# States on the partitions in a selective scan: state sums by few-column matmuls, delta*u spread by DMA

## The chip, the cores and the metric

The kernel runs on one core of a Trainium2 chip. The metric is the time on the device in microseconds (us), lower is better. Lines such as L342 are lines of the kernel before. PE is the matmul engine (PEld its weight loads), DVE, ACT and POOL are the vector, scalar and GpSimd engines, SP issues the transfers.

## What is computed

The input is 8 images of 96 channels and 64x64 positions. A layer of group norm, layer norm, in_proj, depthwise convolution and Silu gives 192 inner channels per image. Then comes the selective scan, over 4096 positions in each of four directions (by rows, by columns, and both reversed), with 16 states per channel. In the reference, cut to this:

```python
def step(h, t):
    u_t, d_t, B_t, C_t = t
    dA = jnp.exp(d_t[..., None] * A)
    h = dA * h + (d_t * u_t)[..., None] * B_t[:, :, None, :]
    y = jnp.einsum('bkdn,bkn->bkd', h, C_t)
    return (h, y)
```

Here `u` is the convolved image in the direction's order, `d` (delta) is a softplus of a low-rank projection of u, B and C are projections of u to 16 values per position, and A is a constant per direction, channel and state. The four directions' y are put back into the image's order and added, with D*u; then follow a norm over the 192 channels, a gate, out_proj and the residual, attention without softmax, and a quantised FFN. All of the scan is in float32.

## The kernel before, in words

The images are handled in four pairs, one after the other, each in four stages: `front` (norms, in_proj, convolution), `scan`, `back` (norm, gate, out_proj), `tail` (attention, FFN). Two images share three tiles of 128 partitions with channels on the partitions: tile 0 is channels 0 to 127 of image 0, tile 1 the same of image 1, tile 2 the last 64 channels of both.

`scan` (L229) goes over 32 steps, four directions times 8 chunks of 512 positions. A step has three tiles T and 16 states n, and each (step, T, n) is a unit; a pair has 1536 units, and a unit's work has 128 channels on the partitions and 512 positions along the free dimension:

- `unit_a` (L318): two bf16 matmuls with a selection matrix spread row n of B and of C over the partitions (L322, L324). ACT makes `da = exp(delta * A)` with A as a per-partition scale (L326). DVE multiplies B by delta*u in PSUM (L329). ACT copies C to SBUF (L331).
- `unit_b` (L336): DVE's scan instruction gives the states h (L342), POOL multiplies them by C (L344), ACT keeps the last column for the next chunk (L347).
- `unit_c` (L350): PE adds the 16 states' products into one PSUM bank with an identity matrix (L352); after the 16th, DVE adds the bank to the running sum of the directions in SBUF (L357, L362).

The units are software-pipelined by hand (L369 to L390): `unit_a` of unit i, `unit_b` of i-1, `unit_c` of i-3. The projections of the next step (`project`, L260; `step_size`, L281, with softplus put together from Relu, Abs, Exp and Ln and three POOL operations) are put in between. In the columns' directions, `view` (L239) reads the image with a stride of 64 elements. All data between the steps stays in SBUF; SP has almost nothing to do in the scan: the weights `xw` and `dtw` of each direction (L256, L258).

`back` reads the sum y and the gate z chunk by chunk; `mix` (L400) forms means over the 192 channels with matrices that respect the three-tile layout. In `back`, po is made of a matmul with 128 rows (L442) and one with 64 rows (L443), the latter on partitions 0 to 63 for image 0 and 64 to 127 for image 1. `tail` holds f32 matmuls with few columns: `pk` (L486, 192 columns), `pm` (L495, 96 columns). At the start, L50 loads the constants, among them `sel` (128 rows of 12,288 bytes), `wkv` (97 rows of 768 bytes), `alog` (128 of 512) and `gmat` (96 of 384), before x is loaded (L139).

Of the kernel before, what the change touches and what calls it, by code (L numbers as in the profile page):

```python
# [30 lines left out]
HG = 4  # L31
LOGEXP = "natural_log_exp_and_others"

# Two images share three 128-partition tiles of the 192 inner channels:
#   tile 0: image 0, channels 0..127      tile 1: image 1, channels 0..127
#   tile 2: channels 128..191 of image 0 (partitions 0..63) and of image 1 (64..127)
# [3 lines left out]
def vss_attn_ffn(ctx: ExitStack, tc: tile.TileContext, a: dict):  # L40
# [12 lines left out]
    # one table set for all but Silu  # L53
# [10 lines left out]
    c192 = load("c192", [128, 6, 128])  # L64
    j192 = load("j192", [128, 6, 128])
    sel = load("sel", [128, 3, NS, 128], BF16)
# [4 lines left out]
    inb = load("inb", [128, 2, 2])  # L71
# [3 lines left out]
    ds = load("ds", [128, 2, KD])  # L75
    onw = load("onw", [128, 2])
    onb = load("onb", [128, 2])
    woT = load("woT", [128, 2, DIM])
# [6 lines left out]
    # A = -exp(A_log); the sum over the directions of D, as all four read the same u  # L85
    amat = load("alog", [128, KD, 2, NS])
    nc.scalar.activation(amat, amat, AF.Exp)
    nc.vector.tensor_scalar(amat, amat, -1.0, None, ALU.mult)
    dsum = const.tile([128, 2], F32, name="dsum")
    nc.vector.tensor_reduce(dsum, ds, mybir.AxisListType.X, ALU.add)  # L90

    # FFN weights and biases in the 5-bit exponent, 2-bit mantissa format
# [26 lines left out]
    def front(pair, xi, zs, ybuf):  # L119
        with ExitStack() as st:  # L120
# [53 lines left out]
            # Silu from here on, in a table set of its own  # L174
            for b in range(2):
                xt = xts[b]
                lo = slice(64 * b, 64 * b + 64)
                for c in range(NCH):
                    cs = bass.ts(c, F)
                    r0 = c * ROWS  # L180
                    for j in range(2):
                        pm = ps.tile([128, F], F32, name="pm", tag="ps")
                        nc.tensor.matmul(
                            pm, winT[:, j * DI : j * DI + 128], xt[:, cs], start=True, stop=True
                        )
                        pl = ps.tile([128, F], F32, name="pl", tag="ps")
                        nc.tensor.matmul(
                            pl[lo], winT[:, j * DI + 128 : (j + 1) * DI], xt[:, cs],
                            start=True, stop=True,
                        )  # L190
                        if j == 0:
                            nc.scalar.activation(
                                pad[b][:, r0 + 1 : r0 + 1 + ROWS, 1 : HH + 1],
                                pm.rearrange("p (h w) -> p h w", w=HH),
                                AF.Identity, bias=inb[:, 0, 0:1],
                            )
                            nc.scalar.activation(
                                pad[2][lo, r0 + 1 : r0 + 1 + ROWS, 1 : HH + 1],
                                pl[lo].rearrange("p (h w) -> p h w", w=HH),
                                AF.Identity, bias=inb[lo, 0, 1:2],  # L200
                            )
                        else:
                            zt = tmp.tile([128, 2, F], F32, name="zt")
                            nc.scalar.activation(zt[:, 0], pm, AF.Silu, bias=inb[:, 1, 0:1])
                            nc.scalar.activation(
                                zt[lo, 1], pl[lo], AF.Silu, bias=inb[lo, 1, 1:2]
                            )
                            nc.sync.dma_start(zs[b, :, cs], zt[:, 0])
                            nc.sync.dma_start(zs[2, lo, cs], zt[lo, 1])

            for T in range(3):
                for c in range(NCH):
# [9 lines left out]
                    silu = nc.scalar.activation(  # L222
                        xi[T][:, bass.ts(c, F)], pc, AF.Silu, bias=convb[:, half(T) : half(T) + 1]
                    )
            with tc.issue_after(silu.ins):
                nc.scalar.preload_act_table_set(LOGEXP)

# [1 line left out]
    def scan(xi, y):  # L229
        with ExitStack() as st:  # L230
            wk = st.enter_context(tc.tile_pool(name="wk", bufs=2))
            pr = st.enter_context(tc.tile_pool(name="pr", bufs=1))
            wt = st.enter_context(tc.tile_pool(name="wt", bufs=3))
            psb = st.enter_context(tc.tile_pool(name="psb", bufs=3, space=PSUM))
            psc = st.enter_context(tc.tile_pool(name="psc", bufs=2, space=PSUM))
            psy = st.enter_context(tc.tile_pool(name="psy", bufs=2, space=PSUM))
            psm = st.enter_context(tc.tile_pool(name="psm", bufs=1, space=PSUM))

            def view(t, k, c):  # L239
                """Chunk c of an image in the order of direction k (before its flip)."""  # L240
                if k % 2 == 0:
                    return t[:, bass.ts(c, F)].rearrange("p (h w) -> p h w", w=HH)
                return t.rearrange("p (h w) -> p w h", w=HH)[:, bass.ts(c, ROWS), :]

            def rows(t):
                return t.rearrange("p (h w) -> p h w", w=HH)

            steps = []
            for k in range(KD):
                order = range(NCH) if k < 2 else range(NCH - 1, -1, -1)  # L250
                steps += [(k, c, i == 0) for i, c in enumerate(order)]
            xw, dtw, S, dts, delta, du = {}, {}, {}, {}, {}, {}

            def weights(k):
                xw[k] = wk.tile([128, 2, 3, 128], F32, name="xw")
                nc.sync.dma_start(xw[k], a["xw"][k])  # L256
                dtw[k] = wk.tile([128, 3, 128], F32, name="dtw")
                nc.sync.dma_start(dtw[k][32:44], a["dtw"][k])  # L258

            def project(s, g):  # L260
                """B (g = 0, with the step's low rank) or C: rows 0..31, 64..95 and 96..127 of S
                get the high, middle and low bfloat16 parts, whose sum is the float32 value."""
                k, c, _ = steps[s]
                if g == 0:
                    S[s] = pr.tile([128, 2, F], BF16, name="S", bufs=2)
                pt = psm.tile([128, F], F32, name="pt", tag="m")
                for T in range(3):
                    nc.tensor.matmul(  # L268
                        pt, xw[k][:, g, T, :], view(xi[T], k, c), start=(T == 0), stop=(T == 2)
                    )  # L270
                Sg = S[s][:, g]
                nc.scalar.activation(Sg, pt, AF.Copy)  # L272
                R = pr.tile([128, F], F32, name="R")
# [32 lines left out]
            def feed(s, T):  # L306
                """What must have run before tile T of step s, in parts."""
                if s >= len(steps):
                    return []
                k, _, first = steps[s]  # L310
                parts = []
                if T == 0:
                    if first:
                        weights(k)
# [368 lines left out]
```

## Time and profile before

| what | value |
|---|---|
| median of 3 runs | 16,712.39 us (16,696.8 to 16,720.28) |
| span of the profiled execution, first to last instruction | 16,699.4 us; it lies among the three runs, and no other time of it is given |
| `front` of the first pair, up to its first projection | 430 us |
| `scan` of the first pair | 3359 us |
| `back` of the first pair | about 130 us |
| busy share of DVE, PE, POOL, ACT | 76%, 84%, 59%, 59% |
| instructions of PE | 32,636 matmuls and as many weight loads |
| data moved by DMA | 106 MB, 6 GB/s over the span |

A group's row reads: line, engine, operation, output <- inputs, shape, count | busy us, mean ns of one | idle time of the engine just before them and what ended it. A window's row gives each engine's busy time in that stretch, then the granted share of PE's clock, the share of the 16 DMA engines that was busy, and GB/s. A row of the waits names who waited for whom, us in total, how often, and the longest.

### The profile page before, as it was taken

The numbers are of one execution on the slowest core, as the hardware profiler recorded it, in microseconds if no ns is written. First come the engines' busy times: TensorE is split into PE (matmuls) and PEld (weight loads), VectorE is DVE, ScalarE is ACT, GpSimd is POOL, SyncE is SP. The second block draws the span as 40 slices with busy tenths as digits, with TensorE's granted clock in tenths as the row PEclk, the third lists the DMA queues.
The fourth block names the chain that finished last, engine by engine and source line by source line (L and its number), as shares of the span: only waits on it lengthen the run. The fifth ranks groups of instructions, "written<-read, shape, count | busy, mean of one in ns | idle before, by whom it ended". The sixth has DMA issues, their size and how long they took to land. (4 is left out here: it accounts for less than half of the span.)

```text
span 16699.4 us, 126308 instructions
## 1 busy us (share of the span) xinstructions
PE 14068.0 (84%) x32636; PEld 4820.2 (29%) x32640; DVE 12648.8 (76%) x14809; ACT 9813.3 (59%) x17754; POOL 9871.6 (59%) x7738
## 2 busy tenths in 40 slices
PE   8888888888988888888898888888889888888888
PEld 2222222223222222222332222222233222222223
DVE  0898899883189889988318988998830898899883
ACT  2666666663266666666326666666632666666663
POOL 0677777772067777777106777777710677777771
PEclk9999999997799999999779999999977999999997
DMA  1000000000000000000000000000000000000001
GB/s 31 2 2 1 2 1 1 1 1 29 24 2 2 1 1 1 1 1 0 30 24 2 2 0 2 1 1 1 1 30 26 0 2 0 2 1 1 1 1 31
DMA packets 48735, 106.06 MB, mean 6 GB/s; under 512 B 7075, under 2 KB 7940, under 8 KB 47108
## 3 DMA queue, kind: packets, MB, share of 16 engines
q1 hardware_dynamic: 48004, 97.97, 2.0%
q8 instruction: 256, 4.19, 0.1%
q14 instruction: 475, 3.89, 0.1%
HBM read 60.21 MB, written 37.75 MB: 6 GB/s over the span
## 5 line engine op out<-in xcount | busy, mean ns | idle before, releaser
L344 POOL TENSOR_TENSOR hc<-h,cc 128x512 f32<-128x512 f32 x6144 | 7831.6, 1280 | 3405.2 <-DVE h L342 2561.7
L352 PE MATMUL py<-hc,ident 128*128 128x512 f32 x12288 | 7244.3, 673 | 1992.9 <-POOL hc L344 1968.2
L342 DVE TENSOR_TENSOR_SCAN h<-da,st,pb 128x512 f32<-128x512 f32 x5376 | 6839.4, 1272 | 11.3
L331 ACT ACTIVATE cc<-pcc 128x512 f32<-128x512 f32 x6144 | 3665.9, 597 | 3446.6 <-POOL hc L344 2798.5
L329 DVE TENSOR_TENSOR pb<-pb,du 128x512 f32<-128x512 f32 x6144 | 4184.9, 681 | 1296.2 <-PE pb L322 1268.9
L326 ACT ACTIVATE da<-delta,c_alog 128x512 f32<-128x512 f32 x6144 | 4414.6, 719 | 497.2 <-DVE h L342 461.7
L352 PEld LDWEIGHTS py<-hc,ident 128*128 128x128 f32 x12288 | 2131.0, 202 | 4978.2 <-POOL hc L344 4475.7
L322 PE MATMUL pb<-S,c_sel 128*128 128x512 bf16 x6140 | 2449.9, 399 | 145.1 <-DVE h L342 141.8
L324 PE MATMUL pcc<-S,c_sel 128*128 128x512 bf16 x6144 | 2348.9, 398 | 5.2 <-POOL S L279 2.5
L279 POOL TENSOR_TENSOR S<-R,S 32x512 bf16<-32x512 f32 x256 | 295.7, 1155 | 1838.5 <-DVE S L278 948.1
L324 PEld LDWEIGHTS <-c_sel 128*128 128x128 bf16 x6144 | 628.6, 102 | 2303.6 <-issue 2250.3
L274 DVE TENSOR_TENSOR R<-pt,S 64x512 f32<-64x512 f32 x256 | 177.8, 695 | 1307.3 <-ACT S L272 1300.0
L322 PEld LDWEIGHTS <-c_sel 128*128 128x128 bf16 x6144 | 631.4, 103 | 1777.1 <-issue 1772.9
L268 PE MATMUL pt<-xi,xw 128*128 128x512 f32 x1536 | 1125.5, 825 | 21.1 <-DMA xw<-in_xw_dram 9.9
L342 DVE TENSOR_TENSOR_SCAN h<-da,pb 128x512 f32<-128x512 f32 x768 | 924.6, 1209 | 5.9
L217 PE MATMUL pc<-y,diag 128*128 128x512 f32 x1728 | 748.1, 595 | 0.0
L544 POOL TENSOR_TENSOR ot<-t,y 96x512 f32<-96x512 f32 x64 | 73.5, 1149 | 951.7 <-DVE y L542 936.7
L300 POOL TENSOR_TENSOR delta<-delta,u 128x512 f32<-128x512 f32 x384 | 486.7, 1267 | 155.2 <-DVE u L299 155.2
L303 POOL TENSOR_TENSOR du<-delta,xi 128x512 f32<-128x512 f32 x384 | 535.5, 1394 | 21.3
L301 POOL TENSOR_TENSOR delta<-delta,r 128x512 f32<-128x512 f32 x384 | 486.6, 1267 | 30.1
L222 ACT ACTIVATE xi<-pc,c_convb 128x512 f32<-128x512 f32 x96 | 66.0, 687 | 681.9 <-PE pc L217 681.9
L285 PE MATMUL ptd<-dts,dtw 12*128 12x512 f32 x768 | 439.7, 652 | 25.1 <-ACT e L292 21.2
(115 smaller groups left out, 8068.9 us busy)
## 6 DMA issues: line engine op xcount, KB each, us to landing
z<-zs SPq DMA_DIRECT2D x32, 768.0 KB, 4.9
zs<-zt SPq DMA_DIRECT2D x64, 256.0 KB, 2.0
xt<-in_x_dram SPq DMA_DIRECT2D x8, 1536.0 KB, 9.4
xr<-in_x_dram SPq DMA_DIRECT2D x32, 384.0 KB
out_dram<-ot SPq DMA_DIRECT2D x64, 192.0 KB, 2.1
zs<-zt SPq DMA_DIRECT2D x64, 128.0 KB
xw<-in_xw_dram SPq DMA_DIRECT2D x16, 384.0 KB, 3.1
c_sel<-in_sel_dram SPq DMA_DIRECT2D x1, 1536.0 KB
```

Source lines behind the costliest of these rows:

```text
L217: nc.tensor.matmul(pc, diag[:, half(T), t, :], pad[T][:, r0 + dy : r0 + dy + ROWS, dx : dx + HH], start=(t == 0), stop=(t == 8),)
L268: nc.tensor.matmul(pt, xw[k][:, g, T, :], view(xi[T], k, c), start=(T == 0), stop=(T == 2))
L300: nc.gpsimd.tensor_tensor(d, d, u, ALU.subtract)
L303: nc.gpsimd.tensor_tensor(rows(q), rows(d), view(xi[T], k, c), ALU.mult)
L322: nc.tensor.matmul(pb, sel[:, T, n, :], S[s][:, 0], start=True, stop=True)
L324: nc.tensor.matmul(pc, sel[:, T, n, :], S[s][:, 1], start=True, stop=True)
L326: nc.scalar.activation(da, delta[s, T], AF.Exp, scale=amat[:, k, half(T), n : n + 1])
L329: nc.vector.tensor_tensor(pb, pb, du[s, T], ALU.mult)
L331: nc.scalar.activation(cc, pc, AF.Copy)
L342: nc.vector.tensor_tensor_scan(hs[:, d], da[:, d], pb[:, d], init, ALU.mult, ALU.add)
L344: nc.gpsimd.tensor_tensor(hc, hs, cc, ALU.mult)
L352: nc.tensor.matmul(py, ident, hc, start=(n == 0), stop=(n == NS - 1))
```

## The change

The scan is rewritten with states on the partitions. A partition is now (image and quarter of its channels, state): 8 groups of 48 channels, group s of image s // 4, times 16 states. A step is 128 positions of one direction (`TC`), and along the free dimension lie 12 channels of 129 places each (128 positions and one place for the start value); four such rows `r` make the 48 channels. The pair has 128 steps.

- `prepare` is a new stage between `front` and `scan`. It computes for every direction and chunk the projections and delta (with one Softplus) and delta*u and writes all to DRAM: `dl`, `du`, `bs`, `cs_`; u itself goes to `us`. In the columns' directions POOL first copies u into that order.
- `scan` reads these back. `load` gets a step's delta, B and C; `fetch` gets `dut`, one row r of delta*u, each group's 12 channels repeated for 16 states. `drive` (POOL) multiplies by B. `decay` (PE) forms delta*A with 32-row matmuls, whose weights hold A, in PSUM, and ACT takes the exponential there. `run` (DVE) scans 6 channels of 129 places in one instruction, the start value restarting each channel. `sums` contracts the states with C: for every position a matmul whose weights are 8 columns and whose moving operand is the 48 channels' states. `store` writes y to DRAM.
- The directions are added in `back`: their y are read back from DRAM with positions on the partitions, and matmuls with the identity transpose and add them. `back` works per image, with channels in two tiles of 96, so `mix` goes.
- At the start, the weights with A in them are laid out through DRAM by many small transfers.

`front` keeps its work; only its gate z is now made in two tiles of 96. `tail` is unchanged. The core of the new code, in this order: the weights of A at the start, a round of `prepare`, the functions of `scan` (the `dut` are a ring of four buffers, `dbu` has two) and its loop, and the sums of the directions in `back` for one chunk and image:

```python
    for k in range(KD):
        aw = wp.tile([128, 16, 128], F32, name="awp", bufs=4)
        nc.gpsimd.memset(aw, 0.0)
        for m in range(8):
            for r in range(NR):
                c0 = 48 * (m % 4) + NI * r
                t = aw[4 * m + r :: 32, r::4, NS * m : NS * m + NS]
                v = ad[k, c0 : c0 + NI].rearrange("(q e) n -> q e n", e=3)
                nc.sync.dma_start(t[:, 0:3], v)
                nc.sync.dma_start(t[0::2, 3], v[1::2, 0])
        nc.sync.dma_start(awd[k], aw)
...
    nc.scalar.activation(S[:76], pt[:76], AF.Copy)
    nc.sync.dma_start(bs[k, :, cs], S[0:32])
    nc.sync.dma_start(cs_[k, :, cs], S[32:64])
    for T in range(3):
        nc.tensor.matmul(pq, dtw[64:76, k, T], S[64:76], start=True, stop=True)
        nc.scalar.activation(d, pq, AF.Softplus, bias=dtb[:, k, half(T) : half(T) + 1])
        nc.vector.tensor_tensor(q, d, u[T], ALU.mult)
...
            def load(s):
                v = dl[k, c].rearrange("s r (q e) t -> q (s r) e t", q=4)
                nc.sync.dma_start(
                    dm[s][:, 0:3].rearrange("p e t -> p (e t)"),
                    v.rearrange("q p e t -> q p (e t)"),
                )
                for q in (0, 2):
                    nc.sync.dma_start(dm[s][32 * q : 32 * q + 32, 3], v[q + 1, :, 0])
                for b in range(2):
                    nc.sync.dma_start(
                        bt[s][64 * b : 64 * b + 64],
                        bs[k, NS * b : NS * b + NS, ts].unsqueeze(0).to_broadcast([4, NS, TC]),
                    )
                for m in range(8):
                    nc.sync.dma_start(
                        cw[s % 3][NS * m : NS * m + NS, m, :], cs_[k, NS * b : NS * b + NS, ts]
                    )
...
            def fetch(g):
                dut[g] = ring.tile([128, NI, TC], F32, name="dut")
                nc.sync.dma_start(
                    dut[g],
                    du[k, c, :, g % 4].rearrange("s i t -> s (i t)").unsqueeze(1)
                    .to_broadcast([8, NS, NI * TC]),
                )
...
            def drive(g):
                t = wk.tile([128, NI * SEG + 1], F32, name="dbu")
                nc.gpsimd.tensor_copy(
                    start, times(hs[s - 1][:, :, r])[:, :, 0 if back else TC - 1]
                )
                nc.gpsimd.tensor_tensor(
                    times(t), dut.pop(g),
                    bt[s].unsqueeze(1).to_broadcast([128, NI, TC]), ALU.mult,
                )
...
            def decay(p):
                t = da[p % 3]
                cut = F - 3 * SEG - 1
                for e, u, x0, x1 in (
                    (0, 0, 0, TC), (4, 1, 0, TC), (1, 0, 0, TC), (5, 1, 0, TC), (2, 0, 0, TC),
                    (3, 1, cut, TC), (3, 0, 0, cut),
                ):
                    q, ii = 2 * hf + u, e - 3 * u
                    lo = e * SEG + 1
                    nc.tensor.matmul(
                        t[:, lo + x0 : lo + x1], aw[k][32 * q : 32 * q + 32, 4 * ii + r, :],
                        dm[s][32 * q : 32 * q + 32, ii, x0:x1], start=True, stop=True,
                    )
                nc.scalar.activation(e, e, AF.Exp)
...
            def run(p):
                nc.vector.tensor_tensor_scan(
                    hs[s][:, w, r][:, d], da[p % 3][:, o : o + W6][:, d],
                    dbu[4 * s + r][:, w][:, d], 0.0, ALU.mult, ALU.add,
                )
...
            def sums(s, f):
                for j in range(8):
                    for q in range(4):
                        t = HQ * q + 8 * f + j
                        nc.tensor.matmul(
                            y[32 * q : 32 * q + 8, 48 * j : 48 * j + 48]
                            .rearrange("p (r i) -> p i r", r=NR),
                            cw[s % 3][:, :, t], h[:, :, t, :], start=True, stop=True,
                        )
                nc.scalar.activation(
                    yev[s][:, 8 * f : 8 * f + 8, :].rearrange("p j e -> p (j e)"),
                    y[:, 0 : 8 * 48], AF.Copy,
                )
...
            for s in range(N + 1):
                for v in range(8):
                    p = 8 * s + v
                    if s < N:
                        if v % 2 == 0:
                            fetch(p // 2 + 3)
                            drive(p // 2 + 1)
                        decay(p + 2)
                        run(p)
                    if s > 0:
                        if v in (1, 2, 4, 5):
                            sums(s - 1, (1, 2, 4, 5).index(v))
                        if v == 6:
                            store(s - 1)
                    if v == 1 and 0 < s < N:
                        load(s + 1)
...
            for k in range(KD):
                for e in range(4):
                    v = ys[k, 4 * b + e]
                    yd = yk[:, k, :, 48 * e : 48 * e + 48]
                    if k % 2 == 0:
                        nc.sync.dma_start(yd, v[cs].rearrange("(p j) e -> p j e", j=4))
                    else:
                        v = v.rearrange("(w g j) e -> w g j e", w=HH, j=4)
                        for g in range(2):
                            nc.sync.dma_start(yd[64 * g : 64 * g + 64], v[:, 2 * c + g])
            for g in range(2):
                for k in range(KD):
                    for j in range(4):
                        nc.tensor.matmul(
                            o, yk[:, k, j, g * DIM : (g + 1) * DIM], ident,
                            start=(k + j == 0), stop=(k + j == KD + 2),
                        )
                nc.vector.scalar_tensor_tensor(
                    yt[:, g], ut[:, g], dsum[:, g : g + 1], py[:DIM], ALU.mult, ALU.add
                )
```

## The prediction

> **What bounds the kernel now.** I read the page's parts 1 and 5 first, then the windows of the first pair of images, then the chain of waits, then the transfers and small matmuls, because the new code lives on those.
>
> ```profile
> PE 14068.0 (84%) x32636; PEld 4820.2 (29%) x32640; DVE 12648.8 (76%) x14809; ACT 9813.3 (59%) x17754; POOL 9871.6 (59%) x7738
> ...
> L344 POOL TENSOR_TENSOR hc<-h,cc 128x512 f32<-128x512 f32 x6144 | 7831.6, 1280 | 3405.2 <-DVE h L342 2561.7
> L352 PE MATMUL py<-hc,ident 128*128 128x512 f32 x12288 | 7244.3, 673 | 1992.9 <-POOL hc L344 1968.2
> ...
> L329 DVE TENSOR_TENSOR pb<-pb,du 128x512 f32<-128x512 f32 x6144 | 4184.9, 681 | 1296.2 <-PE pb L322 1268.9
> L326 ACT ACTIVATE da<-delta,c_alog 128x512 f32<-128x512 f32 x6144 | 4414.6, 719 | 497.2 <-DVE h L342 461.7
> ...
> L342 DVE TENSOR_TENSOR_SCAN h<-da,pb 128x512 f32<-128x512 f32 x768 | 924.6, 1209 | 5.9
> ```
>
> Part 5 shows two DVE passes per unit of 512 positions: the scan at 1.21 to 1.27 us (L342) and the product with delta*u at 0.68 (L329). Every f32 matmul counts twice: 12288 instructions for 6144 units.
>
> ```profile
> 430.40:3789.60 3359.20, 2814.30 (x6722) 952.19 (x6724) 3003.54 (x3392) 2204.48 (x4032) 2400.82 (x1888) 0.94 0.00 1
> ```
>
> This window is one pair's scan; its columns are PE, PEld, DVE, ACT, POOL, the granted clock, and DMA share. DVE is busy 3003.5 of 3359.2 us (89%), so DVE bounds the scan, with PE (84%) close behind and the DMA engines idle. The first L268 and last L352 of the four pairs enclose 3356, 3354, 3353 and 3359 us, 13,422 in all; the rest of the span, 16,699.4 - 13,422 = 3277 us, is front, back, tail and the start; front and tail stay as they are. The median, 16,712.4, is 13 us above the span, and I add those at the end.
>
> **The change, step by step.** One new step is 128 positions of one direction for all 384 channels and 16 states; there are 4 pairs x 4 directions x 32 = 512. In today's kernel that work takes 13,422/512 = 26.2 us.
>
> DVE: L329 goes, and the sums L357 and L362 (374 us in all) go to `back`. What stays is 8 scans of 128x774. One tensor element costs (687 - 254)/416 = 1.04 ns on DVE (rows of 512 and 96 columns, L469 and L503), so the 1209 ns of a scan are 2 x 512 x 1.04 + 143, and 774 columns give 1.75 us; in proportion 1.83. I take 1.79: 14.3 us a step.
>
> POOL: L344's product goes, `drive` comes: 4 of 128x1536, in proportion 3 x 1.28 = 3.84 us, or 3.62 if all but 0.11 us (the smallest POOL row) scales. I take 3.75 and 0.12 for the short start copy: 15.5 us a step. As `dbu` has two buffers, POOL can run one ahead of DVE, and the slower one sets the pace: 15.5.
>
> ACT: 8 exponentials of 768 columns from PSUM at 0.82 us (384 columns took 487 ns and 512 took 597, so 0.86 ns a column), 4 copies at 0.49: 8.5 us, beside the others.
>
> PE, decay: 8 x 7 f32 matmuls of K=32, two instructions each. One instruction of N=512 follows the next after 429 ns, so N=128 takes some 109.
>
> ```profile
> 3805.17 1.10 PE L443 MATMUL po<-g,c_woT 64*96 64x512 f32 x4
> ...
> 3975.52 1.47 PE L486 MATMUL pk<-c_wkv,tn 97*128 97x192 f32 x8
> 3976.92 0.58 PE L495 MATMUL pm<-kv 128*96 128x96 f32 x4
> ...
> 1041.19 1.02 PE L268 MATMUL pt<-xi,xw 128*128 128x512 f32 x2
> ...
> 1344.99 1.88 PE L268 MATMUL pt<-xi,xw 128*128 128x512 f32 x2
> ```
>
> These are timeline lines. The first is four instructions on partitions 0 to 63 and 64 to 127 in 1.10 us, where two in a row (fourth line) take 1.02: matmuls on different row groups run at the same time. `decay` alternates two row groups and two PSUM banks, so I count 4 x 218 ns = 0.9 us a run, 7.2 a step; without overlap 12.3. That is the upper end.
>
> PE, sums: 128 f32 matmuls of 8 weight columns and N=48 replace L352: 256 pairs of weight load and matmul. Lines two and three bound them. Eight pairs of N=192 take 1.47 us, less the last one's length of 0.33 and over seven distances 163 ns a pair; at that slope N=48 takes 41. Four pairs of N=96 take 0.58, less 0.25 over three distances 111 ns, the first weight load in it. Lines four and five are one matmul with a contiguous and with a strided moving operand: strided costs nearly twice. The sums read runs of four contiguous values, nearer to the contiguous row. I take 45 ns: 11.5 us; ends 7 (overlap, as the row groups show it) and 28 (111 ns). With 1.5 for changes of shape PE has some 20 us a step, in slices behind DVE.
>
> [...]
>
> DMA: delta*u, spread 16-fold, is 4 transfers of 128 rows of 6144 bytes a step, where before there was nothing. The question is on how many of the 16 engines.
>
> ```profile
> 6.50:9.50 3.00, 0.00 (x0) 0.00 (x0) 0.00 (x0) 0.00 (x0) 0.00 (x0) 1.00 0.95 360
> 17.45:17.75 0.30, 0.00 (x0) 0.00 (x0) 0.00 (x0) 0.00 (x0) 0.00 (x0) 1.00 0.07 26
> ...
> SPq L50 <- DMA c_sel<-in_sel_dram: 4.5, 1, 4.5
> ...
> SPq L110 <- DMA c_wkv<-in_wkv_dram: 2.3, 1, 2.3
> ```
>
> The last two columns of the windows are the share of 16 engines and GB/s. While `sel` (128 rows of 12,288 bytes) lands, all engines work, at 360 GB/s; while `wkv` lands, whose 97 rows no number up to 16 divides, the share is 0.07, one engine, at 26 GB/s. So a transfer is dealt out evenly by its outer count. The source of `dut` counts 8 groups outermost, then 16 repeats: 8 engines, I conclude, with 16 and 1 as ends. One engine's 26 GB/s gives 6144 bytes in 0.235 us, and 16 of them on each of 8 engines 3.76 us a transfer, 15.0 a step. `dm` counts 4 outermost: 32 rows of 1536 bytes on 4 engines, 2.1 us; `bt` the same way 0.9; `cw` and stores 1.2. The lowest engines, if they serve all of these, carry 19.2 us a step.
>
> [...]
>
> On top comes SP. It waits in the last two lines for the transfer eight before the one it wants to issue (`ds` for `sel`, `b2` for `wkv`), so eight may be open. SP issues one in 0.47 us; 21 a step are 10 us, hidden, but `load` puts 13 short ones between two `dut`: the late `cw` wait for the `dut` and `dm` before them, and the next `dut` comes behind them. I estimate 0.7 until such a one has landed and five issues at 0.47: 3 us without work for the engines, 22 us a step. `store` waits on SP for the copy of the sums with the next `dut` behind it; three `dut` fetched ahead cover that. POOL then idles 6 us a step, which also covers PE's delays. **Scan: 512 x 22 = 11,264 us**, and 4 fills of 20.
>
> `prepare`: 32 rounds a pair. Per round PE 12 instructions at 429 ns = 5.1 us, ACT 0.6 + 3 x 0.69, SP 10 issues = 4.7 us, and 3072 packets of 512 bytes on 16 engines at 27 ns (the trace's packets of `alog`, 512 bytes each) = 5.2 us. I take 6.0; with 17 us for `us`, 209 a pair: **+836** in all, none of it beside the scan, which needs its pool space. Ends 600 and 1500 (writes of 512 bytes into DRAM do not occur in this trace; if Softplus and Copy needed a table each, 64 loads of 1.28 us a pair would add 330). What it replaces, `step_size`, lay in the scan's 13,422.
>
> `back`: 64 rounds. 27 transfers x 0.47 = 12.7 us of SP, 8192 packets of 192 bytes at an estimated 16 ns (`gmat`'s 384 bytes took 22) on 16 engines = 8.2, PE 64 short instructions at 110 ns and 16 of 429 = 14. I take 15: 960 us against today's 4 x 130 = 520: **+440**; ends +200 and +1500.
>
> The start: 256 small transfers for the weights of A, 8 to 40 more: some 280 x 0.47 = **+130**, as SP loads x after them.
>
> Sum: 3277 + 11,264 + 80 + 836 + 440 + 130 = 16,027, and 13 around it: **16,040 us**. The change breaks even at (16,699 - 4763)/512 = 23.3 us a step, only 6% above 22.
>
> **The rivals.** (a) `dut` runs on 16 engines, or the bubble is hidden: POOL sets 15.5, with PE's slices some 16.5 to 19: 13,200 to 14,500. For it: POOL's row; against: the 97-row load. 0.17. (b) PE becomes the bound: the sums cost the strided rate, twice 41 = 82 ns a pair, 21.0 + 7.2 + 1.5 = 29.7 us a step: 20,000 us. It decides from (23.3 - 8.7)/256 = 57 ns a pair on. For it: strided operands cost twice in L268, and writes into PSUM are strided too; against: runs of four are contiguous, and overlap may help. 0.18. (c) The engines are slower on repeated rows: x, in 16 KB rows, came at 242 GB/s on 16 engines, 15 each, so 6.5 us a `dut`, 33 us a step, 21,700 us; a third of that loss already gives 25.7 and 17,900. For it: x's row; against: `sel`'s. 0.23. (d) As forecast, 20 to 23.2 us a step: 15,000 to 16,650. 0.40.
>
> **Numbers.** What this kernel's measurement can tell from no change is 0.2%. Faster: (a) and (d), 0.57. Same 0.02. Slower: (b) and (c), 0.41. The range is 13,400 to 20,200, leaving out the ends of (a), (b) and (c), about 0.2; the forecast's own is 15,000 to 16,650.
>
> **What would show it.** Right: in the scan DMA share 0.4 to 0.5 without gaps, `drive` on POOL waiting for `dut` some 6 us a step, scans at 1.75 to 1.83 us, a step of 22. Wrong: POOL without gaps (a); DVE and ACT waiting for `da` from PE, sums' pairs above 57 ns (b); `dut` packets well above 0.235 us (c); or `prepare` and `back` longer than 209 and 240 us a pair.

## The result and the profile after

The changed kernel takes 21,829.96 us (median of 4 runs, 21,796.41 to 21,843.67), the kernel before beside it 16,712.32: the ratio is 1.306 with a 95% interval of 1.304 to 1.308. The prediction of 16,040 us was wrong in sign, and its range ended at 20,200. The profiled execution spans 21,815.2 us, 5,115.8 more than before.

Stage by stage, each part reaching from one kind of instruction in the traces to the next, sums over the four pairs (the forecast counted from the first L268; here its scan is compared with the time from first to last scan instruction, and the 102 us between the two ways of counting are put ahead of the scan):

| part | forecast change, us | measured change, us |
|---|---|---|
| scan, first to last DVE scan (13,320 before) | -2,056 (to 11,264) | +3,036 (to 16,356) |
| `front`, from the load of x to its last convolution | 0 | -207 |
| between front and scan: `prepare` and the fill | +814 | +1,125 |
| the start, up to the load of x | +130 | +159 |
| `back` | +440 | +788 |
| `tail` | 0 | +215 |
| sum | -672 | +5,116 |

So 5,092 of the 5,788 us between forecast and measurement lie in the scan: a step takes 16,356 / 512 = 31.9 us instead of 22. The shorter `front` was not forecast. Its in_proj, 128 matmul instructions before and after, took 125 us in the second pair of the kernel before:

```profile
4287.00:4412.00 125.00, 125.00 (x130) 25.55 (x128) 1.23 (x2) 45.77 (x66) 0.00 (x0) 0.50 0.16 48
```

In the changed kernel it took 65 us at a granted clock of 0.93 instead of 0.50; why the clock stood higher is not shown. The second line here is `prepare` of the same pair:

```profile
5650.00:5715.00 65.00, 65.00 (x130) 19.52 (x129) 1.23 (x2) 47.07 (x68) 0.00 (x0) 0.93 0.32 91
5901.00:6174.00 273.00, 258.07 (x384) 71.29 (x384) 69.94 (x102) 83.92 (x131) 24.89 (x24) 0.69 0.79 208
```

The page of the changed kernel, parts 1 and 5:

```profile
PE 14699.9 (67%) x199680; PEld 11211.1 (51%) x199680; DVE 8134.3 (37%) x5946; ACT 6186.5 (28%) x8746; POOL 7594.0 (35%) x4286
...
L444 PE MATMUL da<-dm,aw 32*128 32x128 f32 (+2 forms) x57344 | 7686.2, 419 | 6020.3 <-DVE h L459 5824.7
L459 DVE TENSOR_TENSOR_SCAN h<-da,dbu 128x774 f32<-128x774 f32 x4096 | 7031.2, 1758 | 9436.1 <-POOL dbu L421 9391.7
...
L421 POOL TENSOR_TENSOR dbu<-dut,bt 128x1536 f32<-128x1536 f32 x2048 | 7040.7, 3438 | 9114.5 <-DMA dut<-du 8537.4
...
L473 PE MATMUL yp<-h,cw 128*8 128x48 f32 x131072 | 3032.9, 279 | 56.1 <-issue 36.0
```

Read the last columns from the bottom up: DVE's scan (L459) waits 9,392 us for POOL's product (L421), and that waits 8,537 us for `dut`; before, DVE was busy 89% of the scan. PE waits for DVE. The chain ends at the transfer. Windows of the changed kernel (PE, PEld, DVE, ACT, POOL, granted clock, DMA share, GB/s): the first pair's scan; a stretch without `dut`; and one full of it.

```profile
814.00:4874.00 4060.00, 2603.32 (x46806) 2337.04 (x46806) 1755.76 (x1023) 1061.16 (x1529) 1832.26 (x1023) 0.50 0.44 119
3023.50:3029.50 6.00, 4.52 (x88) 3.82 (x84) 2.02 (x2) 2.08 (x3) 3.58 (x2) 0.50 0.18 55
3010.00:3016.00 6.00, 6.00 (x154) 5.41 (x152) 2.84 (x3) 2.08 (x3) 3.60 (x2) 0.50 0.53 122
```

The third shows half of the 16 engines at work, as forecast, but 122 GB/s from 8.5 engines are 14.4 each, where 26 was forecast. The second is the hole between two steps: for 6 us no `dut` moves, only short transfers. From 2000 to 4000 us the packets of 6144 bytes (a row of `dut` each, but for the 32 of the stores among 544 a step) take 365 ns in the median and 364 in the mean; the 5th, 25th, 75th and 95th percentiles are 234, 266, 451 and 482 ns. POOL's products start 6.2, 5.9, 6.6 and 13.3 us apart: three `dut` behind one another, then the hole. SP's waits show what makes the hole (L369 to L383 are `dm`, `bt` and `cw` in `load`):

```profile
SPq L374 <- DMA dut<-du: 5478.5, 988, 7.6
SPq L369 <- DMA dut<-du: 2413.6, 500, 8.5
SPq L383 <- DMA dut<-du: 1898.3, 505, 6.3
```

`load`'s short transfers wait for the `dut` issued before them, and the next `dut` stands behind them, as the prediction had it.

### The profile page after: what moved, and what is told of

Read it like the earlier page. It is cut to its first block, busy times and chain, and to the rows that moved or that the text cites. A ratio compares the mean times of both kernels' runs of the same rounds, so it can differ in the third digit from the quotient of the medians.

```text
span 21815.2 us, 451580 instructions
## 1 busy us (share of the span) xinstructions
PE 14699.9 (67%) x199680; PEld 11211.1 (51%) x199680; DVE 8134.3 (37%) x5946; ACT 6186.5 (28%) x8746; POOL 7594.0 (35%) x4286
## 5 line engine op out<-in xcount | busy, mean ns | idle before, releaser
L444 PE MATMUL da<-dm,aw 32*128 32x128 f32 (+2 forms) x57344 | 7686.2, 419 | 6020.3 <-DVE h L459 5824.7
L459 DVE TENSOR_TENSOR_SCAN h<-da,dbu 128x774 f32<-128x774 f32 x4096 | 7031.2, 1758 | 9436.1 <-POOL dbu L421 9391.7
L444 PEld LDWEIGHTS da<-dm,aw 32*128 32x128 f32 x57344 | 6840.5, 322 | 6648.2 <-DVE h L459 6197.4
L421 POOL TENSOR_TENSOR dbu<-dut,bt 128x1536 f32<-128x1536 f32 x2048 | 7040.7, 3438 | 9114.5 <-DMA dut<-du 8537.4
L449 ACT ACTIVATE da<-da 128x768 f32<-128x768 f32 x4096 | 3256.3, 795 | 10882.8 <-PE da L444 10872.2
L473 PE MATMUL yp<-h,cw 128*8 128x48 f32 x131072 | 3032.9, 279 | 56.1 <-issue 36.0
L473 PEld LDWEIGHTS yp<-h,cw 128*8 128x8 f32 x131072 | 2557.4, 125 | 510.3 <-issue 424.1
L478 ACT ACTIVATE yev<-yp 128x384 f32<-128x384 f32 x2048 | 1005.7, 491 | 1370.8 <-PE yp L473 1361.3
L561 PE MATMUL py<-ident,yk 128*96 128x128 f32 x4096 | 540.0, 290 | 82.0 <-DMA yk<-ys 79.8
L317 PE MATMUL pq<-S,dtw 12*128 12x512 f32 x768 | 531.8, 821 | 2.1 <-ACT delta L321 2.1
```

The lines of the kernel that those rows point to most:

```text
L317: nc.tensor.matmul(pq, dtw[64:76, k, T], S[64:76], start=True, stop=True)
L421: nc.gpsimd.tensor_tensor(times(t), dut.pop(g), bt[s].unsqueeze(1).to_broadcast([128, NI, TC]), ALU.mult,)
L444: nc.tensor.matmul(t[:, lo + x0 : lo + x1], aw[k][32 * q : 32 * q + 32, 4 * ii + r, :], dm[s][32 * q : 32 * q + 32, ii, x0:x1], start=True ...
L449: nc.scalar.activation(e, e, AF.Exp)
L459: nc.vector.tensor_tensor_scan(hs[s][:, w, r][:, d], da[p % 3][:, o : o + W6][:, d], dbu[4 * s + r][:, w][:, d], 0.0, ALU.mult, ALU.add,)
L473: nc.tensor.matmul(y[32 * q : 32 * q + 8, 48 * j : 48 * j + 48] .rearrange("p (r i) -> p i r", r=NR), cw[s % 3][:, :, t], h[:, :, t, :], s ...
```

## The experiments

The theory after the result: the scan is bound by the fetch of `dut`, whose packets take 0.364 us instead of 0.235, and by the hole. Against it stands PE as the bound (rival b). Why the packets are slow was open; rival (c) said repeated rows. In what follows, "packets" are those of 6144 bytes from 2000 to 4000 us, and "step" is four distances of POOL's products there. Each experiment was timed once, e6 four times; the four runs of the changed kernel lie within 47 us of one another. e1, e2, e10, e12, e14, e17, e19 and e20 fetch other rows than the scan needs, so their times say what a form of the transfer is worth and are not those of a usable kernel. The edits are shortened: "..." marks what is left out, `<-` stands for the transfer into a tile, and `rows` are the rows of delta*u in DRAM, 6144 bytes each.

### Whose rows, how many engines

e1: eight engines, but every packet from a row of its own. e2: 128 neighbouring rows as one plain transfer, for which all 16 engines work. In what was expected, Repeat stands against Places, a conjecture by which the time of the packets depends on which partitions are written at the same moments.

```diff
-    dut[g], du[k, c, :, g % 4]...unsqueeze(1).to_broadcast([8, NS, NI * TC]),
+e1  dut[g], rows[o : o + 136].rearrange("(a b) f -> a b f", b=17)[:, 0:NS],
+e2  dut[g], rows[o : o + 128],
```

> Two theories of why a 6144-byte packet of dut takes 365 ns in the changed kernel and not 235, and a dut 6.5 us and not 3.8. Repeat: reading the same row 16 times is slow. [...] Here dut still goes over 8 engines into the same places, but each partition gets a row of its own (other rows of delta*u, so the scan computes with wrong values). Repeat expects packets of 235 ns and about 16,500 us (a step of 23 us); Places expects no change: 365 ns, 21,800 us.

> dut is read as 128 rows one after the other, outer count 128, so over 16 engines (wrong values again, as in the kernel with rows of their own). Places and Repeat expect packets of 235 ns, a dut of 1.9 us, and POOL (3.65 us per drive) as the next bound with the wait behind load's short transfers left: a step of 17 to 20 us, 14,000 to 15,600 us in all. A third theory, that this memory traffic as a whole is limited to some 120 GB/s, expects no change.

e1: 21,012 us, packets 340 ns in the mean, step 30.4. Own rows hardly help: the repeated rows of rival (c) fall. e2: 15,366 us, step 19.5, median packet 234 ns, with nothing changed but the fetch. Its window in a stretch full of `dut`:

```profile
3016.00:3020.00 4.00, 4.00 (x91) 3.62 (x90) 2.76 (x2) 1.29 (x2) 1.77 (x1) 0.50 1.01 412
```

Sixteen engines at 25.5 GB/s each: no limit of the total traffic slows the changed kernel's 122 GB/s.

### Fewer engines, and places 32 partitions apart

e8: two transfers of 64 partitions on four engines each; e9: 32 to 95 on four, the two ends on two each; e10: outer count 2, two groups of 64 partitions.

```diff
+e8  for o in (0, 4): dut[g][NS * o : NS * o + 64] <- du[k, c, o : o + 4, ...] x [4, NS, NI * TC]
+e9  for o, n in ((2, 4), (0, 2), (6, 2)): dut[g][NS * o : NS * (o + n)] <- ... x [n, NS, NI * TC]
+e10 dut[g] <- rows[o : o + 130].rearrange("(a b) f -> a b f", b=65)[:, 0:64]
```

> dut in two transfers of 64 partitions, each with an outer count of 4 and so on 4 engines, in blocks 0-15, 16-31, 32-47, 48-63 (and 64 higher). Each engine carries 32 packets a dut. Places expects that the pairs 32 apart still halve each other although only 4 engines run: packets of 365 to 460 ns, a dut of 12 to 14 us, a step near 55, some 32,000 us. A limit of the traffic as a whole (120 GB/s, of which four engines at 26 ask for 104) expects 235 ns, a dut of 7.5 us, a step of 37, 24,000 us.

> dut in three transfers: partitions 32 to 95 on 4 engines, whose blocks are not 32 apart, then 0 to 31 and 96 to 127 on 2 engines each. Engines 0 and 1 carry 48 packets a dut. Places expects most packets at 235 ns (some slower where a next transfer overlaps), so a dut of about 11.5 us although more packets lie on one engine than in the kernel with two transfers: faster than that one by several ms. A limit of the traffic as a whole expects it slower than that one: 48 against 32 packets per engine, 11.5 against 7.5 us.

> dut from rows of its own (wrong values) with an outer count of 2: engine 0 writes partitions 0 to 63, engine 1 writes 64 to 127, always 64 apart, 64 packets each. In the kernels with four engines at most, packets took 238 ns, so 32 apart does not collide. [...] If what slows the eight engines is their number (120 GB/s for the lowest eight together), packets take 235 ns, a dut 15 us, the whole some 37,000 to 40,000 us.

e8 26,593 us, between its two expectations, packets 275 ns in the mean, median 238; e9 33,455, also 275 and 238; e10 40,635, 258 and 238. The distances of the products are 7.55 us (32 x 0.235), 11.1 to 12.3 (48 x 0.235 = 11.3) and 15.1 (64 x 0.235): the transfers of one `dut` fall on the same engines, and the outer count sets how many (DMA share 0.26 to 0.27 of 16 in e8, 0.13 in e10). e9 slower than e8 is the opposite of what was expected of the places 32 apart. The large transfer of e9, however, has its groups at partitions 32, 48, 64 and 80, so two pairs of them are 32 apart as well, and no run shows by itself what that distance does. And e8 isn't uniform. Right after the hole, and then later in the same stream:

```profile
3031.00:3035.00 4.00, 2.70 (x22) 2.41 (x20) 0.58 (x1) 1.59 (x2) 0.00 (x0) 0.50 0.26 74
```

```profile
3045.00:3060.00 15.00, 12.00 (x248) 10.73 (x248) 6.86 (x4) 4.16 (x6) 7.05 (x5) 0.50 0.27 108
```

The same four engines move 74 GB/s at first and 108 later. Packet by packet, they start within 13 ns of one another behind the hole. The two or three packets behind the first still take 234 to 238 ns; then one engine takes 484, 342, 349, 475, 502, 358, 356, 471 ns and so on, in a cycle of four rows, the others alike; after some 6 to 12 us one after the other falls to 238 and stays there. In the changed kernel the packets, taken eight at a time in the order of their starts from behind the hole on, go through such a cycle of four too: 325, 389, 470 and 451 ns in the mean of the eight (medians over the 61 whole steps from 2000 to 4000 us). The eight start within 305 ns of one another in the median, and the packets leave the cycle, at 236 to 246 ns, for short stretches only.

### The edits that should repair it

e3: partitions p = 8n + m, so that the states are outermost and 16 engines work (and what depends on that order). e4: C's eight short transfers leave `load` and go, 3, 3 and 2 at a time, behind later `dut`. e5: the preload of the table of exp and ln, behind the last Softplus.

```diff
+e3  .unsqueeze(0).to_broadcast([NS, 8, NI * TC])
+e4  if v in (3, 5, 7) and 0 < s < N: spread_c(s + 1, {3: (0, 1, 2), 5: (3, 4, 5), 7: (6, 7)}[v])
+e5  with tc.issue_after(last.ins): nc.scalar.preload_act_table_set(LOGEXP)
```

> Partitions ordered state first, group second (p = 8n + m), so that dut's source counts 16 repeats outermost, then 8 groups: 16 engines with 8 packets each, same data, same result. From the run with 128 plain rows (3.68 us a drive, POOL's own pace) I expect POOL as the bound between the loads even if each packet stays at 365 to 410 ns (8 of them 2.9 to 3.3 us): a step of 18 to 21 us, 14,700 to 16,300 us, and DVE waiting some 5 us a step. If 16 engines don't help (a limit of 120 GB/s whenever rows repeat), 21,000 us or more.

> As the changed kernel, but the eight short transfers of C are issued three, three and two at a time behind the later dut instead of all between two dut. Theory of eight open transfers: SP waits for the transfer eight before, so the run of 13 short ones drains the dut queue once a step and costs 6 us; spread, the drive distances should become even, 6.3 to 7 us, a step of 28 us or less, 19,300 to 20,200 us. Theory that the engines are simply busy (short packets beside dut): the step stays at 32 to 33 us, 21,800 us.

> The preload of the table with Exp and Ln is issued after the last Softplus instead of wherever it was put. The 384 table loads of 1.28 us in back and tail (492 us of ACT) should go. If they lie on the chain of these stages, 300 to 490 us less (21,300 to 21,500 us) and back and tail shorter by 40 to 50 us each a pair; if ACT has room there, no change. The scan stays as it is.

e3: 16,646 us, above the range expected; step 22.0; distances 3.65 to 3.69 us, POOL's own pace, and 10.3 at the hole; yet packets of 418 ns on 16 engines. e4: 17,289 us, step 23.1, faster than expected: the distances are 4.3 to 7.8 us, so the hole of 6 us is all but gone, and the packets take 302 ns in the mean and 247 in the median. A stretch of e4 full of `dut`:

```profile
3024.00:3028.00 4.00, 4.00 (x98) 3.40 (x101) 3.27 (x2) 1.49 (x3) 3.38 (x3) 0.50 0.53 208
```

That is the form of the changed kernel, 8 groups of 16 rows on half of the engines, at 208 GB/s instead of the 122 above. It may be that the short transfers between the `dut` put the engines out of step; e18 tried this. e5: 21,129 us. It takes away the table loads, of which the groups of the changed kernel show these in the tail:

```profile
L621 ACT ACT_TABLE_LOAD x128 | 164.2, 1283 | 2.3
L622 ACT ACT_TABLE_LOAD x128 | 164.2, 1283 | 2.3
```

Ln and Exp changed the table each time, since the preload came too early; with e5 a pair's tail takes 265 us instead of 320, as long as in the kernel before (266). `back`, with 128 loads, got hardly shorter. Some 420 us that e5 gained in the scan (packets 351 ns) were not expected, and I can't explain them.

### Everything together, and PE

e6 is e3, e4 and e5 in one; e7 is the changed kernel with each matmul of the sums issued twice.

> The three single edits together: partitions ordered so that the fetch of dut runs on 16 engines, C's eight transfers spread behind the later dut, the table preload held until the last Softplus. If the fetch and the hole behind C are what the scan waits for, and they add up, POOL's four products (3.4 to 3.6 us each, 207 ns for the start copies) set the pace: 15 to 17 us a step instead of 31.8, so 21,830 - 512 x 15 to 16.8, less some 250 for the tables: 13,000 to 13,900 us. If the packets of a 16-engine fetch stay at 0.42 to 0.44 us and collide more once nothing pauses them, the fetch itself takes 3.5 to 4 us and the step 16 to 18: up to 14,500. If something behind the transfers (PE with its sums at the lowered clock, or SP's 21 issues) is the next limit, 18 us a step or more: above 14,800.

> Every matmul of the sums is issued twice (the second writes the same values again), so PE gets 256 more instructions with their weight loads in a step: 5.9 us at the 23 ns that they took. If the fetch sets the pace, PE's slices lie in time in which DVE and POOL wait for dut, and the time stays within 1% of 21,830. If PE, at the lowered clock, is the limit or close behind, it grows by up to 512 x 5.9 = 3,000 us, to 24,800.

e7: 21,789 us; 131,072 more matmuls cost nothing. But the granted clock rose from 0.50 to 0.68 and PE's busy time fell, from 1,277 of 2000 us in the changed kernel (first window here) to 1,206 (e7, last window below), so e7 gave PE no longer work and decides little by itself.

```profile
1000.00:3000.00 2000.00, 1276.58 (x22936) 1144.99 (x22932) 855.90 (x499) 519.78 (x749) 892.08 (x498) 0.50 0.44 118
```

That PE doesn't bound the changed kernel is shown by e2, where the same work of PE fits into 19.5 us a step at the same clock; so rival (b) falls. e6: 15,257 us (15,251 to 15,272), 0.913 of the kernel before, interval 0.912 to 0.915: faster than both kernels, but 19.7 us a step, not 15 to 17. Windows of e6, then of e7, over the same stretch:

```profile
1000.00:3000.00 2000.00, 1907.37 (x37254) 1717.58 (x37246) 1388.91 (x811) 841.69 (x1214) 1471.31 (x810) 0.50 0.85 192
```

```profile
1000.00:3000.00 2000.00, 1205.84 (x38968) 1092.76 (x38972) 861.62 (x500) 508.76 (x747) 898.07 (x500) 0.68 0.44 119
```

In e6 PE is busy 95% at a granted clock of 0.50; in e2 it is the same (96%, 0.50, 19.5 us). With the doubled sums of e7 the clock was higher. So I asked whether more work raises it in e6: e15 adds a 128x128 matmul of 248 columns, read by nobody, before each `decay`; e16 doubles the sums.

```diff
+e15 nc.tensor.matmul(t[:, 776:1024], ident, aw[k]...[:, 0:248], start=True, stop=True)
+e16 for _ in range(2): nc.tensor.matmul(y[32 * q : ...
```

> The three edits together, and before each decay one more f32 matmul of 128x128 by 248 columns into columns of the same tile that nobody reads: two instructions, some 0.41 us at the full clock and 0.83 at half of it. If TensorE sets the pace because its clock stands at 0.50, and denser matmuls raise it, decay falls from 1.65 us and more to 0.9, and 8 x (0.9 + 0.41) + 4 x 0.8 to 1.2 of sums are 13.7 to 15.3 us: POOL and the fetch set the pace again, 16 to 18 us a step and 13,300 to 14,400 us. If the clock stays at 0.50, TensorE has 8 x 0.83 = 6.6 us more to do in a step: 26 us, 18,600. If TensorE isn't the bound, the time stays within 2% of 15,257.

> The three edits together, with each matmul of the sums issued twice. If TensorE's clock sets the pace and rises as it did when the sums were doubled in the changed kernel (0.68), the sums take 512 x 11 ns = 5.6 us at the full clock and decay 7.2: the step is between 16 and 19.5 us and the time 13,400 to 15,200, no longer than with half of the work. If the clock stays at 0.50, 256 more instructions of 19 to 23 ns are 5 to 6 us a step more: 17,800 to 18,300.

e15: 19,865 us, 28.8 a step; e16: 18,701, 26.4 a step; both took longer than any of their expectations. Their windows:

```profile
1000.00:3000.00 2000.00, 1991.46 (x25936) 1512.23 (x25924) 954.98 (x540) 561.59 (x810) 984.21 (x541) 0.52 0.59 127
```

```profile
1000.00:3000.00 2000.00, 1591.28 (x47156) 1441.64 (x47145) 1039.37 (x606) 620.21 (x908) 1102.57 (x607) 0.66 0.66 144
```

e15's eight matmuls (some 1.1 us each, where 0.83 was expected) are in the step in full, 9.1 us: PE bounds e6. The clock didn't follow the busy share, 99.6% at 0.52. In e16 it rose to 0.66, and still the step grew, though PE was busy only 80%; PE's idle stretches there reach 5.7 us, and for most of that time the trace shows nothing that it waited for. That a higher clock would help e6 is not shown.

### Why the packets are slow

e12: two transfers of 64 partitions, 8 engines, 8 rows each (groups 8 partitions apart). e14: the changed kernel's places, from neighbouring rows. e17: 16 engines, 8 rows each, own rows. e18: the changed kernel with a short transfer on four engines behind three `dut` of four. e19: plain 128 rows, every second one. e20: plain, one row 128 times.

```diff
+e12 for p0 in (0, 64): dut[g][p0 : p0 + 64] <- rows...rearrange("(a b) f -> a b f", b=9)[:, 0:8]
+e14 dut[g] <- rows[o : o + 128].rearrange("(b a) f -> a b f", a=8)
+e17 dut[g] <- rows[o : o + 144].rearrange("(a b) f -> a b f", b=9)[:, 0:8]
+e18 gap <- rows[o : o + 12].rearrange("(a b) f -> a b f", b=3)[:, 0:2, 0 : NI * TC // 2]
+e19 dut[g] <- rows[o : o + 256 : 2]
+e20 dut[g] <- rows[o : o + 1].to_broadcast([128, NI * TC])
```

> The fetch of dut as two transfers of 64 partitions, each with outer count 8 and 8 rows inside, rows of its own instead of repeated ones (wrong values): eight engines as before, and as many packets on each, but engines that go in step write partitions 8 apart instead of 16. If the places 16 apart that the engines write in step cost the packets their time, the packets fall from 0.34 to 0.365 us to near 0.24, a dut to 3.9 us, and with some 2 us more for SP's extra issues the step is 24 us: 17,500 to 18,500. If it is eight engines going in step, wherever they write, the packets stay at 0.33 to 0.37 and the time between 20,700 and 22,500.

> The fetch of dut as one transfer on eight engines to the same places as in the changed kernel, but from 128 neighbouring rows, of which engine e reads rows e, e+8, e+16 and so on (wrong values): engines in step read eight neighbouring rows of 6144 bytes, 49 KB in all, instead of rows 24 KB or 104 KB apart. If the places in DRAM that engines read in step cost the packets their time, they fall to near 0.24 us and the time to 16,500 to 17,500. If it lies in what they write, or in eight engines going in step, the packets stay at 0.33 to 0.37 and the time between 20,500 and 22,000.

> dut fetched by one transfer with outer count 16 and 8 rows inside, every packet from a row of its own (wrong values): as many engines and places as with the plain 128 rows, but rows in 16 groups with a gap between the groups. If reading one row from 16 engines at a time was what slowed the packets to 0.42 us with the other order of partitions, they take 0.24 to 0.29 us here and the kernel 15,200 to 15,700 us. If it is the form of the transfer (groups with rows inside), whatever they read, the packets take 0.40 to 0.45 and the kernel 16,300 to 17,000 us.

> The changed kernel with one short transfer more behind three of a step's four dut: outer count 4, two packets of 3072 bytes on each of four engines, into a tile that nobody reads. It puts four of the eight engines behind the others. If eight engines going in step is what costs, the packets of 6144 bytes fall from 0.365 to 0.24 to 0.31 us and the time to 18,000 to 20,000, although SP issues three more a step. If going in step has nothing to do with it, packets stay at 0.34 to 0.38 and the time between 21,800 and 23,000.

> dut fetched by one transfer of 128 rows in one level, as the plain rows were, but every second row (wrong values): the rows are 12 KB apart and do not form one stretch. If the one level is what keeps the packets at 0.235 us, the median stays there, the mean below 0.30, and the time between 15,200 and 15,700 us. If it was the one stretch of DRAM, the packets take 0.40 to 0.45 us as those of the grouped transfer on 16 engines, and the time is 16,300 to 17,000.

> dut fetched by one transfer that reads one and the same row 128 times, in one level (wrong values). If repeated reading costs by itself, as the rival with the repeated rows had it, the packets take 0.40 us or more and the time is above 16,300. If only the grouping of the rows costs, the median packet takes 0.235 us and the time is 15,200 to 15,700.

| run | form | engines | packets: median, mean, ns | step, us | time, us |
|---|---|---|---|---|---|
| e12 | groups | 8 | 339, 350 | 31.1 | 21,391 |
| e14 | groups | 8 | 382, 379 | 32.7 | 21,914 |
| e17 | groups | 16 | 431, 414 | 21.8 | 16,619 |
| e18 | groups | 8 | 353, 351 | 32.2 | 21,845 |
| e19 | plain | 16 | 234, 296 | 19.6 | 15,404 |
| e20 | plain | 16 | 234, 294 | 19.5 | 15,418 |

e12 and e14 show that neither groups 8 partitions apart instead of 16 nor neighbouring rows make the packets fast. A window of e17 full of `dut`, beside e2's above:

```profile
3012.00:3019.50 7.50, 5.70 (x108) 5.04 (x105) 4.00 (x3) 2.88 (x4) 4.46 (x3) 0.50 1.04 243
```

Same 16 engines, same 128 places, own rows in both: 243 GB/s against 412. What differs is the form: 16 groups of 8 rows, or one run of 128. Even one row read 128 times goes at 234 ns in the plain form (e20). So **what slows the packets is that the rows are dealt out in groups**, whatever rows are read; that much is shown. In the changed kernel a group is 16 partitions. It isn't a price of each grouped packet: two engines (e10), e8 after its first microseconds and stretches of e4 move grouped rows mostly at 234 to 247 ns. So it takes several engines that move groups at once, and even then it doesn't always happen.

How they hinder each other is not shown, since the trace has no partition for a packet. For engines that hinder each other when they go in step, some numbers speak: slow packets of 470 to 502 ns, about twice 235 (0.47, an estimate), a cycle of four rows, and 238 ns for e8's four engines once they no longer started together. Others speak against it. e18 had been set up to break the step, and by its own expectation its result (351 ns, 21,845 us) speaks against engines in step as the cause; that its short transfer delays four engines together, and so may leave these four in step, was seen only afterwards. And the first packets behind e8's hole go at 234 ns although the four engines start together. Why e8's engines leave the cycle after some 6 to 12 us, and the eight in the changed kernel only briefly, stays open too.

## Why the prediction was wrong, by its steps

- **The bound before**: DVE, by 89%; no run here touched this reading.
- **DVE and POOL**: right. A scan took 1.758 us (forecast 1.79), POOL's product 3.44 and its start copy 0.21 (3.75 and 0.12).
- **Eight engines**: right, by the DMA share of 0.53 and by e8 and e10, whose outer counts of 4 and 2 went with shares of 0.26 to 0.27 and 0.13.
- **The step that failed**: "One engine's 26 GB/s gives 6144 bytes in 0.235 us, and 16 of them on each of 8 engines 3.76 us a transfer, 15.0 a step." The mean packet took 0.364, so 64 of them a step take 23.3 us. These 8.3 us x 512 = 4,250 us are most of the error. In e2, where 16 engines move the rows in the plain form, the median packet took the forecast 0.234. The price was read off a load on one engine (`wkv`) and off `sel`, which was a plain transfer; neither has engines with groups of rows.
- **The rest of the step**: 31.9 - 23.3 = 8.6 us against 22 - 15.0 = 7.0. The hole and its cause were right (it all but goes in e4), its size somewhat low: 1.6 x 512 = 820 us.
- **PE**: not the bound, as forecast, but by other terms. Its 20 us a step were summed at the full clock; the scan ran at 0.50. There a run of `decay` took 14 instructions of 118 to 127 ns, 1.65 to 1.8 us (0.9 forecast; e7 shows 63 ns and 0.9 us while the clock stood at 1.0), and the sums 19 to 23 ns an instruction, 4.8 to 5.9 us a step (11.5 forecast). The errors cancel by luck: 19.5 to 19.7 us is the step where PE bounds it (e2, e6). At the full clock, with the 11 ns of a stretch of e7, the 256 instructions of the sums would be 2.8 us. The 1.5 us for changes of shape had come from no row; in the changed kernel's scan the sums start 346 ns after the last instruction of `decay`, and `decay` 211 ns after the last of the sums (medians from 1000 to 4500 us, start to start), where neighbours within a run are 127 and 19 ns apart in the mean: an estimate of 1.6 us for the four pairs of changes in a step, at a clock of 0.50.
- **`prepare`**: +1,125 against +814 with the fill. A pair's rounds take 274 to 286 us, not 209: PE is busy 258 of 273 us in the second pair, 8.1 us a round, at a granted clock of 0.69, where 5.1 us were summed at the full clock. The shorter `front` (-207), which was not forecast, hides most of this in the total. **The start**: +159 against +130, nearly right.
- **`back`**: +788 against +440; a round takes 19.0 us instead of 15, PE being busy in 15.6 of them, as 16 rounds show:

```profile
4894.00:5199.00 305.00, 250.17 (x1267) 160.35 (x1268) 75.17 (x106) 75.87 (x90) 0.00 (x0) 0.94 0.67 130
```

- **`tail`**: +215 against nothing, the table loads (e5). I weighed tables for `prepare` alone and did not ask what the moved preload leaves to later stages.
- **The rivals**: (c) had nearly the right price, 33 us a step and 21,700 us, by luck, as its cause was wrong: repeated rows go at 234 ns in e20, own rows at 340 in e1. Its row, x's 16 KB rows at 15 GB/s an engine, was the warning that I gave 0.23. (b) fell by e2. (a), the 16 engines: 16,646 us with the hole left (e3) and 15,257 without it (e6), not 13,200 to 14,500, as PE comes next.

## What to carry to other kernels

A transfer's rate has to be read from a row with the same form, number of engines and rows per engine; one engine alone (26 GB/s for `wkv`) or a plain transfer (0.234 us a row in the median, e2) said nothing here of eight or sixteen engines that move rows in groups (0.364 in the mean in the changed kernel, 0.414 in e17). Sum PE's part of a stage at more than one clock: a stage of small matmuls ran at half of the full one here even when busy 95% of the time, and `prepare` at 0.69. When a stage with another activation table is added, look at every later stage for loads: here they cost 55 us in each tail (e5).

## What the hardware showed unexpectedly

- Sixteen engines moved 412 GB/s to 128 partitions in a plain transfer and 243 in 16 groups of 8 rows (e2, e17); eight engines with groups of 16 rows moved 122 in a stretch of the changed kernel and 208 in one of e4.
- The granted clock stood at 0.50 to 0.52 with PE busy 95 to 99.6% over 2000 us (e6, e15), and was 0.66 to 0.68 with doubled sums (e7, e16). So in these runs the profile's busy share doesn't tell the clock.
- An f32 matmul of 8 weight columns and 48 moving ones took 19 to 23 ns an instruction at half the clock, and 11 in a stretch of e7 with the clock at 1.0, so the sums cost 4.8 to 5.9 us a step where 11.5 had been forecast. The stretch:

```profile
3002.40:3003.80 1.40, 1.40 (x126) 1.40 (x127) 1.00 (x1) 1.07 (x2) 1.40 (x1) 1.00 0.26 79
```

- Ln and Exp, used in turn without a preload that holds both in force, cost ACT 1.283 us each time (the changed kernel, L621 and L622).
